# The last stage of a decoder layer cut into 670 steps, with one order over all token tiles written out for every engine, norms and quotients on ScalarE, and its loads issued behind the first gathers

## The chip, the cores and the metric

The kernel runs on one core of a Trainium2 chip. A core has a matrix engine (TensorE, in the profile PE, with its weight loads as PEld), a vector engine (VectorE, DVE), an engine for activation functions (ScalarE, ACT), a general engine (GpSimd, POOL) and one that mostly issues transfers (SyncE, SP). Each works through its own list of instructions strictly in order; they wait for one another through semaphores. Transfers are issued by SP, ACT and POOL and are carried out by 16 DMA engines that all queues share.

The metric is device time in microseconds (us) of one launch, as the median of several runs. The span is the part of one profiled launch from its first to its last instruction.

## What is computed

One decoder layer on 1024 tokens (4 sequences of 256) of width 256. After a Mamba block and a mixture of experts, three additions with a layer norm each follow:

```
x = layernorm(x + moe(x));  x = layernorm(x + cross_attention(x, ctx));  x = layernorm(x + ffn(x))
# cross attention: 16 heads of 128, 64 keys
q = rmsnorm(x @ Wq, gq);  k = rmsnorm(ctx @ Wk, gk);  v = ctx @ Wv
out = softmax(q k^T / sqrt(128)) v @ Wo
# ffn, 704 wide, with fp8 rounding of x, of the weights and of t
qx, sx = fp8(x[:, idx] / rowmax);  g, u = qx Wg^T, qx Wu^T;  t = silu(g) * u;  y = fp8(t[:, idx2]) Wd^T
```

The kernel folds Wq with the keys into one matrix M for each batch, so that scores come straight from x, and folds the values with Wo, so that the attention output is one product too. The projection x @ Wq is still done, for the norms of q alone.

## The kernel before

Tokens lie in 8 tiles of 128 rows (one row on each partition), in `x_sb`. The stages before the last one are untouched: the Mamba block with its scan (to about 430 us), the folding of keys and the routing, and the mixture of experts, which runs 23 slots of 128 rows and stores each slot's rows in the memory tensor `ys_d` (L1167). SP issues those stores, ACT the last two.

Inside the last slot the pools of the last stage are opened (L1188 to L1203). There SP is given, in this order: the context (`cT_v`), the parts of Wv and Wo for half of the heads (L641 to L647), the whole of Wq (`wq_sb`, 2 MB, L1202) and M of batch 0 (`mb`, 1 MB, L1203). Half of the folded values were computed during the scan and parked in memory (`vw_d`). The other half is computed now by `prep_v` (products `p_vT` at L657 and `p_vw` at L669, copied out by ACT).

Then POOL issues two gathers for each tile, of its two expert rows (`yg`, L1240), with the transfers of the stage between them: the parked values after tile 1 (L1246), the FFN weights after tile 3 (L1215 to L1218), M of batch 1 after tile 5 (L1253). POOL's transfers use eight semaphores in turn, so that the ninth can be issued only when the first has landed.

Each tile goes through five steps in code:

- `combine` (L1231): DVE adds the two gathered rows times their gates to x, and `layernorm` (L73 to L76) follows: statistics, `rsqrt_mean` (two small DVE instructions at L64 and L65 and a square root on ACT at L66) and the scaling on DVE (L76).
- `stage_scores`: x is transposed (L1274, copied out by ACT, L1275). Four projections with Wq (L1280) are squared by ACT (L1285) and summed by DVE (L1286) for the q norm (`rq`, L64 to L66 and L1291). Two products with M give the scores (L1295), which DVE scales (L1302). The softmax follows on whole tiles of 128x1024: maximum on DVE (L1305), subtraction on POOL (L1306), exponential on ACT (L1307), sum and reciprocal on DVE (L1308, L1309), multiplication on POOL (L1310).
- `stage_attend`: transposes (L1321), copies (L1324), eight products with the values (L1327), addition (L1330), layer norm.
- `stage_up`: POOL masks x (L1347). `quantize` takes the row maximum (L1338), scales (L1340), and `round_fp8` rounds to fp8 steps (two DVE instructions, L81 and L84, two POOL instructions, L85 and L86). Transposes (L1351, L1353) and the products `p_gu` with gate and up weights in two halves (L1361) follow; DVE scales both (L1366), ACT does the silu (L1368), DVE multiplies (L1369).
- `stage_down`: quantize again on 704 columns, transposes (L1378), copies (L1381, L1382), the products `p_fo` (L1386), DVE adds (L1391, L1392), layer norm, store (L1394).

The loop runs the tiles in a pipeline: step i does the scores of tile i, the attention of tile i-1, the up part of i-2 and the down part of i-3. Inside this loop a scheduler of the framework decides the order in which each engine gets the instructions; in the parts before it, and in the head of this stage, the order is that of the code (`manual_schedule`). Working tiles are double buffered; PSUM has four small buffers (`ps`) and two large ones (`pw`, shared by scores and `p_gu`).

Of the kernel before, what the change touches and what calls it, by code (L numbers as in the profile page):

```python
# [11 lines left out]
I32 = mybir.dt.int32  # L12
# [34 lines left out]


@with_exitstack
def decoder_kernel(  # L50
# [16 lines left out]

    def layernorm(buf, t, pool):

        st = pool.tile([P, 6], F32, tag="ln_st", name="ln_st", bufs=2)  # L70
        mv = pool.tile([P, 2], F32, tag="ln_mv", name="ln_mv", bufs=2)
        rs = pool.tile([P, 1], F32, tag="ln_rs", name="ln_rs", bufs=2)
        nc.vector.bn_stats(st, buf[:, t, :])  # L73
        nc.vector.bn_aggr(mv, st)
        rsqrt_mean(rs, mv[:, 1:2], 1, EPS_LN)
        nc.vector.tensor_scalar(buf[:, t, :], buf[:, t, :], mv[:, 0:1], rs, sub, mult)  # L76
# [52 lines left out]
    )  # L129
    a_neg = const.tile([P, NC * N], F32, name="a_neg")  # L130
# [506 lines left out]
    def prep_v(vp, groups, put):  # L637


        cT = vp.tile([P, B * S], F32, name="cT_v")  # L640
        nc.sync.dma_start(cT, ctxT)  # L641
        ws = {}
        for q in groups:
            wt = vp.tile([P, HALF], F32, tag="wv_t", name="wv_t", bufs=len(groups))
            nc.sync.dma_start(wt, wv[:, q * HALF : (q + 1) * HALF])
            w2 = vp.tile([P, GQ, D], F32, tag="wo_t", name="wo_t", bufs=len(groups))
            nc.sync.dma_start(w2, wo[q * HALF : (q + 1) * HALF, :].rearrange("(h p) d -> p h d", p=P))  # L647
            ws[q] = wt, w2
        ps = yield
        yield  # L650
        for q in groups:
            wt, w2 = ws.pop(q)
            vT = vp.tile([P, GQ, B * S], F32, tag="vT", name="vT")
            for j in range(0, GQ, 2):
                pt = ps.tile([P, HALF], F32, tag="ps", name="p_vT")
                for o in range(2):
                    nc.tensor.matmul(  # L657
                        pt[:, o * B * S : (o + 1) * B * S], wt[:, (j + o) * HD : (j + o + 1) * HD], cT,
                        start=True, stop=True,
                    )  # L660
                yield
                nc.scalar.copy(vT[:, j : j + 2, :].rearrange("p h s -> p (h s)"), pt)
            for j in range(GQ // 2):
                for b2 in range(B // 2):
                    pt = ps.tile([P, HALF], F32, tag="ps", name="p_vw")
                    for b in range(2):
                        for o in range(2):
                            bb = 2 * b2 + b
                            nc.tensor.matmul(  # L669
                                pt[o * S : (o + 1) * S, b * D : (b + 1) * D],  # L670
                                vT[:, 2 * j + o, bb * S : (bb + 1) * S], w2[:, 2 * j + o, :],
                                start=True, stop=True,
                            )
                    yield
                    put(2 * b2, q * (GQ // 2) + j, pt.rearrange("p (b d) -> p b d", d=D))
# [18 lines left out]
    with tc.manual_schedule(engines={ET.PE, ET.DVE, ET.Activation, ET.Pool}):  # L694
# [4 lines left out]
        for i, (h, c0, n) in enumerate(SL):  # L699
# [14 lines left out]
            if i == M + 2:  # L714
# [9 lines left out]
                early_values = prep_v(vp, range(2), park)  # L724
                next(early_values)
# [12 lines left out]
            if i == M + 2:  # L738
                early_values.send(ps1)
# [361 lines left out]
    with ExitStack() as sctx, tc.manual_schedule(engines={ET.PE, ET.DVE, ET.Activation, ET.Pool}):  # L1101
# [70 lines left out]
        for s in range(NSLOT + 1):  # L1172
# [13 lines left out]
            if s == NSLOT - 1:  # L1186
# [7 lines left out]
                mbs = [kvl.tile([P, KD, H * S], F32, tag="mb", name=f"mb{b}", bufs=2) for b in range(2)]  # L1194
# [3 lines left out]
                late_values = prep_v(  # L1198
                    vp, range(2, H // GQ), lambda b, pr, v: nc.scalar.copy(vw_sb[:, b : b + 2, pr, :], v)
                )  # L1200
                next(late_values)
                nc.sync.dma_start(wq_sb, wq.rearrange("(k p) c -> p k c", p=P))  # L1202
                nc.sync.dma_start(mbs[0], m_d[0].rearrange("p k h s -> p k (h s)"))  # L1203
# [9 lines left out]
    def load_ffn():  # L1213
        for j in range(2):
            nc.gpsimd.dma_start(wgu[j], wgu_d[j])  # L1215
            nc.gpsimd.dma_start(wdn[j], wdn_d[j])
        nc.gpsimd.dma_start(sgu_row, sgu_d.unsqueeze(0).to_broadcast([P, 2, I]))
        nc.gpsimd.dma_start(sdn_row, sdn_d.unsqueeze(0).to_broadcast([P, D]))  # L1218
# [3 lines left out]
    with ExitStack() as xctx:  # L1222
        wk2 = xctx.enter_context(tc.tile_pool(name="wk2", bufs=2, side="right"))
        ps = xctx.enter_context(tc.tile_pool(name="psX", bufs=4, space=PSUM))
        pw = xctx.enter_context(tc.tile_pool(name="psW", bufs=2, space=PSUM))
        ygs = {}

        def combine(t):
            if t < NT:
                for j in range(2):  # L1230
                    nc.vector.scalar_tensor_tensor(  # L1231
                        x_sb[:, t, :], ygs.pop((t, j)), g2[:, j, t : t + 1], x_sb[:, t, :], mult, add
                    )
                layernorm(x_sb, t, wk2)

        with tc.manual_schedule(engines={ET.PE, ET.DVE, ET.Activation, ET.Pool}):
            for t in range(NT):
                for j in range(2):
                    y = ygs[t, j] = wk2.tile([P, D], F32, tag="yg", name="yg", bufs=2 * NT)
                    nc.gpsimd.indirect_dma_start(  # L1240
                        out=y, out_offset=None, in_=ys_d,
                        in_offset=bass.IndirectOffsetOnAxis(ap=yrow_i[:, j, t : t + 1], axis=0),
                    )

                if t == 1:
                    nc.gpsimd.dma_start(  # L1246
                        vw_sb[:, :, 0 : H // 4, :].rearrange("p b h d -> p b (h d)"),
                        vw_d.rearrange("b p h d -> p b (h d)"),
                    )
                if t == 3:  # L1250
                    load_ffn()
                if t == 5:
                    nc.gpsimd.dma_start(mbs[1], m_d[1].rearrange("p k h s -> p k (h s)"))  # L1253
            late_values.send(ps)
            for _ in range(8):
                next(late_values)
            combine(0)
            for _ in range(3):
                next(late_values)
            combine(1)  # L1260
            run(late_values)
        mb_of = dict(enumerate(mbs))

        def load_batch(b):
            mb_of[b] = kvl.tile([P, KD, H * S], F32, tag="mb", name="mb", bufs=2)
            nc.sync.dma_start(mb_of[b], m_d[b].rearrange("p k h s -> p k (h s)"))

        def stage_scores(t):

            mb = mb_of[t * P // L]  # L1270
            x1T = wk2.tile([P, KD, P], F32, tag="x1T", name="x1T")
            pt = ps.tile([P, HALF], F32, tag="ps", name="p_x1T")
            for k in range(KD):
                nc.tensor.transpose(pt[:, k * P : (k + 1) * P], x_sb[:, t, k * P : (k + 1) * P], ident)  # L1274
            nc.scalar.copy(x1T.rearrange("p k t -> p (k t)"), pt[:, 0 : KD * P])  # L1275
            ssq = wk2.tile([P, H], F32, tag="ssq", name="ssq")
            for q in range(H // GQ):
                pq = ps.tile([P, HALF], F32, tag="ps", name="p_q")
                for k in range(KD):
                    nc.tensor.matmul(  # L1280
                        pq, x1T[:, k, :], wq_sb[:, k, q * HALF : (q + 1) * HALF],
                        start=(k == 0), stop=(k == KD - 1),
                    )
                q2 = wk2.tile([P, HALF], F32, tag="q2", name="q2")
                nc.scalar.activation(q2, pq, AF.Square)  # L1285
                nc.vector.tensor_reduce(  # L1286
                    ssq[:, q * GQ : (q + 1) * GQ], q2.rearrange("p (h d) -> p h d", d=HD), AX.X, add
                )
            rq = wk2.tile([P, H], F32, tag="rq", name="rq")
            rsqrt_mean(rq, ssq, HD, EPS_A)  # L1290
            nc.vector.tensor_scalar_mul(rq, rq, 1.0 / math.sqrt(HD))  # L1291
            psc = pw.tile([P, 2, HALF], F32, tag="pw", name="p_sc")
            for c in range(2):
                for k in range(KD):
                    nc.tensor.matmul(  # L1295
                        psc[:, c, :], x1T[:, k, :], mb[:, k, c * HALF : (c + 1) * HALF],
                        start=(k == 0), stop=(k == KD - 1),
                    )
            v = wk2.tile([P, H, S], F32, tag="v", name="v")
            full = [P, H, S]  # L1300
            st = wk2.tile([P, 2, H], F32, tag="st", name="st")
            nc.vector.tensor_tensor(  # L1302
# [94 lines left out]
        for i in range(NT + 3):  # L1397
            if i < NT:
                if i % 2 == 0 and 2 <= i // 2 + 1 < B:
                    load_batch(i // 2 + 1)  # L1400
# [78 lines left out]
```

## Time and profile before

| | |
|---|---|
| median of 3 runs | 846.73 us (846.08 to 849.98) |
| the profiled execution | 845.77 us, of which its span 843.6 us |
| PE, DVE, ACT, POOL busy over the span | 81%, 67%, 40%, 46% |
| last `ys_d` store issued | 610.4 us |
| first gather issued | 619.2 us |
| first projection of tile 0 | 631.7 us |
| last attention product of tile 7 ends | 805.8 us |
| span ends | 843.6 us |

A line of a timeline holds the start and the length in us, the engine, the source line, the instruction, its output and inputs, how many, and in brackets the idle time before it with what ended it. A line of windows holds a stretch, its length and the busy time of each engine in it, with the granted TensorE clock behind it (1.00 is full speed) and the share of the DMA engines.

### The profile page before, as it was taken

What the parts mean: (1) busy time and instruction counts of PE and PEld (TensorE: products, weight loads), DVE (VectorE), ACT (ScalarE), POOL (GpSimd) and SP (SyncE); (2) the same over time, 40 slices, a digit from 0 to 9 for tenths busy, and PEclk for the clock granted to TensorE, in tenths of its full rate; (3) what the DMA queues carried; (4) which work ended last, traced back from release to release, by engine and by line L of the source; (5) the groups of instructions that cost most, each with busy time, mean ns of one, the idle gap of its engine ahead of it and who ended that gap; (6) DMA issues with size and microseconds to landing.
All of it is one profiled execution on the core that took longest, in us unless ns stands there. A gap on an engine that the chain in (4) does not pass through costs nothing.

```text
span 843.6 us, 8099 instructions
## 1 busy us (share of the span) xinstructions
PE 683.3 (81%) x2449; PEld 379.0 (45%) x2449; DVE 563.2 (67%) x959; ACT 341.2 (40%) x564; POOL 391.2 (46%) x286
## 2 busy tenths in 40 slices
PE   3968877777666985846999999999959898889963
PEld 1533343334333443534555655655624454555531
DVE  4468799998889894564335454456227678788885
ACT  3386654755633533322212211211233455555533
POOL 7039977899766970022012332222045334344451
PEclk9999998999897998878999999999979999999985
DMA  4023222343941526963022554331566101000000
GB/s 155 1 72 84 99 73 65 88 131 118 307 123 50 162 87 219 399 225 110 26 67 23 66 54 50 60 50 45 167 248 248 50 1 50 7 6 7 8 6 19
DMA packets 57579, 80.75 MB, mean 96 GB/s; under 512 B 16033, under 2 KB 37281, under 8 KB 56769
## 3 DMA queue, kind: packets, MB, share of 16 engines
q1 hardware_dynamic: 49360, 62.21, 23.7%
q0 software_dynamic: 3632, 12.78, 7.6%
q10 hardware_dynamic: 4544, 5.24, 1.8%
q8 instruction: 21, 0.34, 0.2%
q14 instruction: 22, 0.17, 0.1%
HBM read 66.45 MB, written 13.77 MB: 95 GB/s over the span
## 4 chain that ended last, share of the span: by engine, by line
PE 46%; DVE 25%; POOL 11%; ACT 6%; issue 5%; DMA 5%; SPq 0%; POOLq 0%; ACTq 0%; DVEq 0%
PE p_gu L1128 12%; PE p_hTb L1158 7%; PE py L692 5%; DVE hs L702 5%; POOL dbx L597 4%; PE p_q L1280 3%; DVE hc L710 2%; PE p_gu L1361 2%; PE p_m L831 2%; DMA mb<-m_d 2%; PE p_cv L269 2%; POOL v L1306 1%; DVE ssq L1286 1%; DMA wk_t<-in_wk_dram 1%; PE p_hTa L1146 1%
## 5 line engine op out<-in xcount | busy, mean ns | idle before, releaser
L702 DVE TENSOR_TENSOR_SCAN hs<-da,dbx 128x1024 f32<-128x1024 f32 x64 | 145.6, 2281 | 20.3 <-POOL dbx L597 10.3
L597 POOL TENSOR_TENSOR dbx<-dtx,bB 128x1024 f32<-128x1024 f32 x64 | 149.5, 2358 | 20.2 <-DVE dtx L385 11.0
L692 PE MATMUL py<-hc,ident 128*128 128x512 f32 x256 | 132.5, 646 | 3.8 <-POOL hc L733 3.8
L1128 PE MATMUL p_gu<-w,xT 128*128 x276 | 119.3, 570 | 2.0 <-ACT xT L1118 2.0
L589 ACT ACTIVATE da<-dt,a_neg 128x510 f32<-128x510 f32 x128 | 87.7, 689 | 42.9 <-DVE hs L702 40.7
L692 PEld LDWEIGHTS py<-hc,ident 128*128 128x128 f32 x256 | 52.0, 205 | 99.8 <-issue 88.4
L1128 PEld LDWEIGHTS p_gu<-w,xT 128*128 128x128 f32 x276 | 50.0, 194 | 44.2 <-issue 34.9
L1158 PE MATMUL p_hTb<-w2r,hT 128*128 (+1 forms) x276 | 67.8, 387 | 0.0
L608 PE MATMUL pC<-bc,sel 96*128 96x512 bf16 x50 | 20.1, 401 | 56.3 <-DVE hc L710 55.5
L710 DVE TENSOR_TENSOR hc<-hs,pC 128x1024 f32<-128x1024 f32 x50 | 61.1, 1221 | 4.7
L1280 PE MATMUL p_q<-wq_sb,x1T 128*128 128x512 f32 x128 | 59.0, 615 | 4.0 <-ACT x1T L1275 3.5
L1158 PEld LDWEIGHTS p_hTb<-w2r,hT 128*128 128x128 f32 (+1 forms) x276 | 50.4, 189 | 18.4 <-issue 7.8
L1139 DVE TENSOR_TENSOR h<-sg,p_gu 128x704 f32<-128x704 f32 x23 | 20.4, 887 | 42.5 <-ACT sg L1137 42.5
L1147 ACT COPY hT<-p_hTa 128x512 f32<-128x512 f32 x23 | 13.5, 585 | 83.1 <-PE p_hTa L1146 76.0
L924 POOL DMA_INDIRECT xs<-flat_d,tok_i x23 | 22.6, 983 | 43.4 <-PE p_xT L1116 29.0
L85 POOL TENSOR_TENSOR wgu<-wgu,w_m 128x512 f32<-128x512 f32 (+1 forms) x6 | 7.6, 1267 | 71.3 <-DVE w_m L84 71.3
L1280 PEld LDWEIGHTS p_q<-wq_sb,x1T 128*128 128x128 f32 x128 | 24.5, 196 | 33.9 <-issue 27.7
L1154 DVE COPY hT<-p_hTb 128x128 f32<-128x128 f32 (+1 forms) x46 | 11.1, 282 | 42.3 <-PE p_hTb L1151 42.3
L733 POOL TENSOR_TENSOR hc<-hs,cB 128x1024 f32<-128x1024 f32 x14 | 32.9, 2351 | 11.9 <-issue 8.0
L1361 PE MATMUL p_gu<-wgu,xqT 128*128 128x352 bf16 x128 | 25.8, 367 | 10.5 <-ACT xqT L1353 10.5
L1285 ACT ACTIVATE q<-p_q 128x512 f32<-128x512 f32 x32 | 18.9, 593 | 35.9 <-PE p_q L1280 28.4
L1240 POOL DMA_INDIRECT yg<-ys_d,yrow_i x16 | 15.5, 969 | 38.3 <-DMA mb<-m_d 32.6
(332 smaller groups left out, 1265.7 us busy)
## 6 DMA issues: line engine op xcount, KB each, us to landing
bB<-b_d SPq DMA_DIRECT2D x64, 256.0 KB, 3.2
w<-in_w1T_dram SPq DMA_DIRECT2D x2, 2816.0 KB, 23.3
w<-in_w3T_dram SPq DMA_DIRECT2D x2, 2816.0 KB, 30.2
w2r<-in_w2T_dram SPq DMA_DIRECT2D x8, 640.0 KB, 7.8
m_d<-mst SPq DMA_DIRECT2D x8, 512.0 KB, 4.0
cB<-b_d SPq DMA_DIRECT2D x14, 256.0 KB, 3.5
mb<-m_d SPq DMA_DIRECT2D x3, 1024.0 KB, 4.8
ys_d<-y SPq DMA_DIRECT2D x21, 128.0 KB, 1.7
```

Source lines behind the costliest of these rows:

```text
L589: nc.scalar.activation(das[i % 2][:, j, :, 1:], dt[h][:, c, :].rearrange("p (b l) -> p b l", l=L)[:, :, 1:], AF.Exp, scale=a_neg[:, c * N ...
L597: nc.gpsimd.tensor_tensor(dbxs[i], dtx[h][:, c0 : c0 + 2, :], bBs.pop(i).unsqueeze(1).to_broadcast(two), mult)
L692: nc.tensor.matmul(ys[i][j], ident, hc[:, j, :], start=(n == 0), stop=(n == N - 1))
L702: nc.vector.tensor_tensor_scan(hs, das[i % 2].rearrange("p c b l -> p (c b l)"), dbxs.pop(i).rearrange("p c t -> p (c t)"), 0.0, mult, add,)
L710: nc.vector.tensor_tensor(hcs[i], hv, pcs.pop(i).unsqueeze(1).to_broadcast(two), mult)
L733: nc.gpsimd.tensor_tensor(hcs[i], hv, cBs.pop(i).unsqueeze(1).to_broadcast(two), mult)
L924: nc.gpsimd.indirect_dma_start(out=xs[s], out_offset=None, in_=flat_d, in_offset=bass.IndirectOffsetOnAxis(ap=tok_i[:, s : s + 1], axis=0),)
L1128: nc.tensor.matmul(pt[:, c, 0:w], x[:, k, :], w13[k][:, bass.DynSlice(ex[s], 1), o : o + w].rearrange("p e i -> p (e i)"), start=(k == 0), ...
L1139: nc.vector.tensor_tensor(hs[s], g, v[:, I : 2 * I], mult)
L1158: nc.tensor.matmul(po, hT[:w, i, :], w2r[:w, i, bass.DynSlice(ex[s], 1), :].rearrange("p e d -> p (e d)"), start=(i == 0), stop=(i == NI - 1),
L1280: nc.tensor.matmul(pq, x1T[:, k, :], wq_sb[:, k, q * HALF : (q + 1) * HALF], start=(k == 0), stop=(k == KD - 1),)
L1361: nc.tensor.matmul(pg[:, g, 0:HI], xqT[:, k, :], wgu[j][:, k, g, hs], start=(k == 0 and j == 0), stop=(k == KD - 1 and j == 1),)
```

## The change

Only the last stage changes, and what it needs set up. The loop over tiles is replaced by 670 steps. A step has an engine, an assumed length, the steps it follows and the buffers it uses. `Weave.order` plays the engines through once on the host: again and again it takes the step that can start first (within 0.037 us, the one with the lowest due time in `PLAN` plus the tile's `STARTS`), books its engine for its length and its buffers. An ACT step that needs another function table is charged 0.327 us. The resulting order is emitted under `manual_schedule`, so it is the order in which each engine gets its instructions. The steps of one tile:

- `both`: for tiles 0 and 1 two DVE instructions as before; from tile 2 on ACT multiplies the gathered rows by their gates (`gates`) and POOL adds them in two instructions.
- Norms (`ln0`, `ln1`, `ln2`): DVE statistics; the square root on ACT with eps as its bias; reciprocal and one small instruction on DVE; the scaling of x on ACT, no longer on DVE.
- `rq`: square root straight on the sums on ACT, then one DVE reciprocal.
- The softmax is done in halves of 8 heads, each with its own steps `v`, `max`, `sub`, `exp`, `sum`, `div`, `aT`, `av`.
- `x_f`, `t_f` (the quotients of the quantization) move from DVE to ACT. The scaling of the up half (`s_up`) moves from DVE to POOL, and so does the output's (`y_add`), after ACT has scaled it (`y`). Tile 7 keeps the POOL part of all this on DVE.
- The loads of Wq (in two halves) and of M of batch 0 go from SP to POOL, behind the two gathers of tile 0; the FFN weights and M of batch 1 move forward, behind the gathers of tiles 2 and 3.

```
+    "ps": 4, "pw": 2, "yg": 6, "ln": 4, "x1T": 2, "q2": 2, "nq": 3, "v": 4, "st": 4, "aT": 3, "x_f": 2, "xq": 2,
+    "sx": 4, "xqT": 2, "gu": 4, "tb": 3, "t_m": 2, "tq": 2, "s2": 4, "tT": 2, "y": 2      # buffers of each kind
-                nc.sync.dma_start(wq_sb, wq.rearrange("(k p) c -> p k c", p=P))
-                nc.sync.dma_start(mbs[0], m_d[0].rearrange("p k h s -> p k (h s)"))
...
+        for t in range(NT):
+            for j in range(2):
+                yg[t, j] = Buf("yg")
+                ld["yg", t, j] = w(f"yg.{t}", POOL, 1.25, gather(t, j, yg[t, j]), (), (yg[t, j],), lands=3.5, plan=next(turn))
+            if t == 0:
+                for k in range(KD):
+                    ld["wq", k] = load("wq", wq_sb[:, k, :], wq[k * P : (k + 1) * P, :], ())
+                ld["mb", 0] = load("mb", load_of(0), m_d[0]..., (), (mb_of[0],))
+            if t == 1:
+                ld["vw"] = load("vw", ...)
+            if t == 2:      # wgu 0, wgu 1, sgu
+            if t == 3:      # wdn 0, wdn 1, sdn, mb 1
...
+            if t < 2:
+                s = w(f"both.{t}", DVE, 1.0, both, got, ys, plan=at("both"))
+            else:
+                s = w(f"gates.{t}", ACT, 0.84, gates, got, ys, plan=at("both"))
+                s = w(f"both.{t}", POOL, 1.5, both_added, (s,), ys, plan=at("both"))
+            s = norm(t, 0, s, at("both"))
...
+    # in norm: the last of its four steps
-        nc.vector.tensor_scalar(buf[:, t, :], buf[:, t, :], mv[:, 0:1], rs, sub, mult)
+            return w(f"ln{stage}_out.{t}", ACT, 0.42,
+                lambda: nc.scalar.activation(x, x, AF.Identity, scale=b.tile[:, 7:8], bias=b.tile[:, 8:9]), (s,), (b,), plan=at)
...
-                nc.vector.tensor_tensor(gu, pg[:, :, 0:HI], sgu_row[:, :, hs], mult)
-                nc.scalar.activation(s, gu[:, 0, :], AF.Silu, scale=sx[:, 0:1])
-                nc.vector.scalar_tensor_tensor(tb[:, hs], gu[:, 1, :], sx[:, 0:1], s, mult, mult)
+                s = w(f"g_out.{t}", DVE, 0.46, ... pg.tile[:, 0, 0:HI], sgu_row[:, 0, hi], mult
+                s = w(f"silu.{t}", ACT, 0.59, ... AF.Silu, scale=sx.tile[:, 0:1]), (s,), (gu, sx), "silu", ...
+                s = w(f"s_up.{t}", eng, 0.5 if late else 0.9, ... pv.tensor_tensor(gu.tile, gu.tile, sgu_row[:, 1, hi], mult)
+                halves.append(w(f"tb.{t}", DVE, 0.58, ... pg.tile[:, 1, 0:HI], sx.tile[:, 0:1], gu.tile, mult, mult
...
-            nc.vector.tensor_scalar_mul(f, src, sc[:, 1:2])
+            s = w(f"t_f.{t}", ACT, 0.75, lambda: nc.scalar.activation(tb.tile, tb.tile, AF.Copy, scale=s2.tile[:, 1:2]), ...
...
-            nc.vector.tensor_tensor(y, po[:, 0:D], sdn_row, mult)
-            nc.vector.scalar_tensor_tensor(x_sb[:, t, :], y, sx[:, 0:1], x_sb[:, t, :], mult, add)
+                s = w(f"y.{t}", ACT, 0.42, ... nc.scalar.activation(y.tile, bo.tile[:, 0:D], AF.Copy, scale=s2.tile[:, 0:1] ...
+                s = w(f"y_add.{t}", POOL, 1.5, add_on_pool, (s, ld["sdn"]), (y,), plan=at("fo"))
```

The order that comes out, first as each engine gets it at the beginning of the stage (the number is the tile; `wgu`, `sgu`, `wdn`, `sdn` are FFN weights and scales, `val` a piece of the folded values; `[T]` marks a table load on ACT):

```
POOL yg.0 yg.0 wq wq mb yg.1 yg.1 vw yg.2 yg.2 wgu wgu sgu yg.3 yg.3 wdn wdn sdn mb yg.4 yg.4 both.2 both.3
     yg.5 yg.5 yg.6 yg.6 both.4 sub.0 yg.7 yg.7 both.5 both.6 sub.0 div.0
ACT  val x8 [T] ln0_sqrt.0 val ln0_out.0 val val x1T_out.0 ln0_sqrt.1 val ln0_out.1 gates.2 q_sq.0 x1T_out.1 q_sq.0
     gates.3 q_sq.1 q_sq.0 ln0_sqrt.2 ln0_out.2 gates.4 ln0_sqrt.3 ln0_out.3 q_sq.0 rq_sqrt.0 q_sq.1 x1T_out.2 gates.5
PE   val x11 x1T.0 val q.0 x1T.1 q.0 q.1 q.0 sc.0 sc.0 q.0 q.1 x1T.2 q.1 sc.2 q.2 sc.2 q.2 q.2 q.2 q.1 sc.1 aT.0 aT.0
```

and at its end, from the first `gu.4`:

```
PE   gu.4 gu.4 xqT.5 av.7 fo.3 gu.5 xqT.6 gu.5 fo.2 xqT.7 gu.6 gu.6 tT.4 fo.4 gu.7 gu.7 tT.5 fo.5 tT.6 fo.6 tT.7 fo.7
ACT  [T] silu.4 xqT_out.5 silu.4 x_f.6 y.3 [T] ln1_sqrt.7 xqT_out.6 t_f.4 ln1_out.7 ln2_sqrt.3 [T] silu.5 silu.5 x_f.7
     ln2_out.3 y.2 xqT_out.7 t_f.5 silu.6 silu.6 tT_out.4 [T] ln2_sqrt.2 y.4 t_f.6 ln2_out.2 [T] silu.7 tT_out.5 silu.7
     [T] ln2_sqrt.4 y.5 tT_out.6 t_f.7 ln2_sqrt.5 ln2_out.4 y.6 ln2_out.5 tT_out.7 ln2_sqrt.6 ln2_out.6 ln2_sqrt.7 ln2_out.7
DVE  tb.4 x_ex.6 res.7 ln1_stat.7 tb.4 t_sc.4 g_out.5 ln1_sc.7 ln2_stat.3 g_out.5 xm.7 x_sc.7 ln2_sc.3 t_ex.4 x_ex.7
     x_rd.7 tb.5 tb.5 t_sc.5 g_out.6 g_out.6 t_ex.5 tb.6 ln2_stat.2 tb.6 t_sc.6 ln2_sc.2 g_out.7 t_ex.6 g_out.7 s_up.7 tb.7
     ln2_stat.4 s_up.7 tb.7 t_sc.7 ln2_sc.4 ln2_stat.5 t_ex.7 ln2_sc.5 t_rd.7 ln2_stat.6 ln2_sc.6 y.7 ln2_stat.7 ln2_sc.7
POOL s_up.4 s_up.4 x_rd.6 y_add.3 s_up.5 s_up.5 t_rd.4 y_add.2 s_up.6 s_up.6 t_rd.5 y_add.4 t_rd.6 y_add.5 y_add.6
```

ACT gets 29 table loads from the first square root of the stage on; before it got 33.

## The prediction

> **What bounds the kernel now.** I read the page first, then the windows of the last stage, its PE timeline, the waits, and POOL's and ACT's timelines around its head.
>
> ```profile
> span 843.6 us, 8099 instructions
> PE   3968877777666985846999999999959898889963
> PEclk9999998999897998878999999999979999999985
> ...
> 631.70:805.80 174.10, 155.77 (x596) 88.95 (x596) 138.74 (x307) 90.60 (x145) 73.13 (x57) 0.96 0.13 48
> 805.80:843.60 37.80, 17.40 (x90) 9.46 (x90) 23.54 (x56) 11.24 (x20) 14.24 (x11) 0.69 0.04 14
> ```
>
> From 631.7 to 805.8 PE is the bound: 155.8 of 174.1 us busy (first pair of numbers), DVE 138.7, ACT 90.6, POOL 73.1. The last 37.8 us are a drain: PE is busy 17.4 us, at a clock of 0.69.
>
> ```profile
> 631.72 9.16 PE L1280 MATMUL p_q<-wq_sb,x1T 128*128 128x512 f32 x16 [0.51 <-issue]
> 645.00 7.13 PE L1280 MATMUL p_q<-wq_sb,x1T 128*128 128x512 f32 x16 [0.46 <-ACT x1T L1275]
> 802.03 3.72 PE L1327 MATMUL p_av<-vw_sb,aT 128*128 128x256 f32 x16 [0.37 <-ACT aT L1324]
> 818.26 4.88 PE L1361 MATMUL p_gu<-wgu,xqT 128*128 128x352 bf16 x16 [0.46 <-ACT xqT L1353]
> PE p_gu L1361 <- ACT xqT L1353: 10.5, 8, 2.3
> PE p_fo L1386 <- ACT tT L1381: 5.7, 3, 2.8
> ```
>
> The same 16 projections take 7.13 us warm and 9.16 after an idle stretch; `p_gu` takes 2.56 warm (at 808.6) and 4.88 in the drain. So idle PE is paid for twice. The two waits are the largest of PE within the tile loop.
>
> ```profile
> 610.43 0.33 ACTq L1167 DMA_DIRECT2D ys_d<-y  x1
> 619.17 0.95 POOL L1240 DMA_INDIRECT yg<-ys_d,yrow_i  x1 [32.56 <-DMA mb<-m_d]
> 632.51 0.54 POOL L1216 DMA_DIRECT2D wdn<-wdn_d  x1 [1.00 <-DMA vw_sb<-vw_d]
> 652.17 0.60 ACT L1285 ACTIVATE q<-p_q 128x512 f32<-128x512 f32 x1 [1.12 <-PE p_q L1280]
> 652.78 1.28 ACT L1307 ACT_TABLE_LOAD   x1
> 654.08 1.06 ACT L1307 ACTIVATE v<-v 128x1024 f32<-128x1024 f32 x1
> ```
>
> The first gather starts 8.7 us after the last store, while Wq and M (3 MB on SP) occupy the DMA engines. A POOL transfer waits for the one eight places ahead. A table load costs 1.28 us, with no gap around it.
>
> **PE's work is unchanged.** One tile, by warm rows of the PE timeline: projections 7.13, scores 3.43, attention products 3.72, their transposes 1.05, x transposed 0.30, `xqT` 0.28, `gu` 2.56, `tT` 0.62, `fo` 1.58: 20.67, eight tiles 165.4 us. Before, 12.2 of these lie behind the last attention product, so 153.2 fill 174.1 us: 20.9 lost to waits and cold clock. I call end = S + work up to the last attention product + loss + drain, where S is the time at which an unbroken PE stream would have begun. Before: 631.7 + 153.2 + 20.9 + 37.8 = 843.6.
>
> **The head, S.** With Wq and M off SP, the last store can land about 2 us after 610.4 (other `ys_d` stores on SP: median 1.7); the two gathers of tile 0 issue from 612.5 to 615. From the first gather to the end of the first norm it is 7.7 us now (626.8), so x of tile 0 is ready by about 621. Wq issues at 615, moves from 617.7 (the 2 MB of `vw` also started 2.7 us after issue) at the 400 GB/s that the DMA row shows from 627 to 643, and is there at 623: q.0 could begin 8.7 us earlier than now. But the order ties it to later gathers on the same POOL queue. After 3 MB of Wq and M, yg.1 lands at 626; after 2 MB of parked values, yg.2 at 632; after 2.1 MB of FFN weights yg.3 at 638; yg.4 at 643.5. ACT has `gates.2` ahead of the first `q_sq.0`, so nothing of q.0 is squared until 632.9; PE has x1T.1 behind one q.0 and q.1 behind x1T_out.1 (634). `gates.3` holds ACT to 638.9 and `gates.4` to 644.4. Also wdn waits for `vw` eight places ahead, and `both.2` stands behind yg.4, which holds POOL to about 639. Walking on, PE has done 6 projections and 2 scores (14.1 us) at 644.5 and loses 1.3 after it: S = 644.5 - 14.4 + 1.3 = 631.4; I take 632 for `gates.7`. Ends: 626 if the landings come six us earlier, 635 if each gate adds a stall of one us.
>
> **The middle.** PE work up to the last attention product is 165.4 less what now follows it: fo.3, gu.5, xqT.6, fo.2, xqT.7, gu.6, tT.4, fo.4, gu.7, three more tT and three more fo: 20.2. So 145.2. The other engines, whole stage, by rows:
> - ACT: per tile 7.8 us of steps as before (four squares at 0.59, eight heads' exponentials twice at 0.59, copies, silu) plus 2.1 for three norms (0.2 + 0.50, the row of ACT's scaled copy 128x256), x_f 0.45, t_f 0.76 (the 128x704 silu row), y 0.45, gates 0.9: about 104 with the values; 29 table loads at 1.28 are 37. Sum 141 (106 before).
> - DVE: 16.2 per tile, 7.5 more for tile 7, 2 for `both`: 139 (167 before).
> - POOL: 13.5 for seven tiles (halves of the softmax 1.04 each, the row of 128x512; t_rd 3.36), `both` 9, gathers 20, loads 6: 130 (98 before).
>
> All stay below PE's 165, at 70 to 75% between the head and the drain. Covered steps therefore cost nothing; the cover is PE's next work, which the order supplies (av.3, sc.4 and q.5 stand between one gu and its fo), and gu now comes at least one product behind its xqT, which takes most of the 10.5 us wait away. What is late next: `silu` then `s_up` on POOL then `tb` hold a `pw` buffer some 5 us where one DVE instruction held it; POOL's t_rd in front of s_up adds up to 3.4. And two-port waits stay: the q norm's L64 took 0.16 to 1.49 us (median 0.68) against 0.17 in idle times of POOL, and POOL is now busier. The 32 exponent instructions of the quantizations pay it still (t_m: mean 0.72 against 0.51), the norms no longer. Loss: at least 3 (cold starts alone), at most the 20.9 of now unless a rival below holds; I take 8, nearer the low end since the two largest waits go.
>
> **The drain.** With av.7 ending at 0, walked by the order and the rows: res, statistics, a table load and the square root of tile 7 end at 3.6; xqT.6 and t_f.4 keep ACT until ln1_out.7 at 5.2; xm, x_sc, x_f (behind both silu.5 at 8.0), x_ex, x_rd end at 9.8. PE has run dry at 6.1 and gets xqT.7 at 9.9. tb.5 frees `pw` at 10.4 and 11.0 for gu.6; t_rd.4 and y_add.2 hold POOL to 14.1, s_up.6 to 16.2, so tb.6 and gu.7 come at 17 to 22, on a cold clock. tb.7 at 25, t_sc.7, t_f.7, t_ex.7, t_rd.7 at 31.5; tT.7, tT_out.7 and a cold fo.7 to 36; then y, norm and store as at present (5.6 from the end of `p_fo` to the end of the span) to 41. One table load runs ahead of what it waits for (in the present drain, one at 802.48 does): 40. Bounds: 34 (DVE's 29 us behind av.7 plus 5) and 44. It is no shorter than now because four tiles' FFN remain where two did.
>
> **Sum.** 632 + 145.2 + 8 + 40 = 825.2. The profiled execution took 2.2 more than its span, so 827.4 against its 845.77; the median of the runs is 1.0 above that execution, so **828**.
>
> **A rule against a row.** "ScalarE: Activation LUTs" of the Trainium skill, section What ACT_TABLE_LOAD costs, puts a switch at about 1.28 us for the load and 1.38 for a drain, 2.66 in all. The load agrees with the trace; the drain does not show: the load at 652.78 begins as the square ends and the exponential starts 1.30 later. By the page ACT's 29 switches would be 77 us and its sum some 181, above PE's 165, and ACT the bound; by the row 141.
>
> **Rivals.**
> - *Better cover*: landings early (S 626), loss 4, drain 36: 811.2, so 814. For it: every engine has room. Against: the gates on ACT.
> - *Table loads through PE (slower)*: the order charges 0.33 for a switch that takes 1.28. If each of the 24 loads ahead of the drain arrives 0.96 late on a path for which PE waits, loss grows by 23: 848.2, so 851. It decides once 19 of the 24 pass through (18.4 / 0.96). For it: ACT is at 75% and in order. Against: four `ps` and four `v`, `st`, `gu` buffers let PE run ahead, and a load may run early.
> - *Little gained*: the gates stall the head (S 638) and half of the loads pass through: 842.7, so 845.
>
> **How the numbers follow.** Chances: forecast 0.66, better cover 0.18, table loads 0.10, little gained 0.06. The likeliest gives 828. Its own bounds, not all at one end, make 816 to 841; 811 to 843 takes in most of the better case and leaves out about 0.18. A change within 0.5% (842.5 to 851, about what a measurement of this kernel can tell from none) holds 0.05 of the last case and 0.03 of the slow one: 0.08. The rest of the slow case is slower by more: 0.07. Faster: 0.85.
>
> **What would show it.** First gather near 612.5; q.0 near 623 but its second projection after 629, with ACT's `gates.2` waiting for a DMA until about 632; PE idle below 10 us up to av.7; av.7's end near 785; PE waiting for xqT.7 and tT in the drain of about 40 us; 29 table loads of 1.28. It is wrong if ACT's squares trail PE's projections through the middle (table loads), or if gathers land long before 632 and PE streams from 624.

## The result, and the profile after

The changed kernel takes 843.9 us (median of 20 runs, 840.65 to 850.77) against 846.56 for the kernel before beside it: a ratio of 0.9976, interval 0.9954 to 0.9999. The gain of 0.24% is at the edge of the noise, and by the bound of 0.5% it is no change; 828 was forecast, and 811 to 843 as the range. The profiled execution took 842.04 us with a span of 840.3.

The page of the changed kernel (span, PE's busy tenths and granted clock), and its windows from the first projection to the end of the last attention product (792.4) and from there to the end of the span:

```profile
span 840.3 us, 8206 instructions
PE   3977877867676986745999999999978996998944
...
622.10:792.40 170.30, 148.76 (x542) 83.68 (x541) 108.98 (x252) 105.11 (x184) 90.09 (x98) 0.94 0.18 65
792.40:840.30 47.90, 25.32 (x148) 14.39 (x146) 35.47 (x79) 25.08 (x46) 24.78 (x23) 0.70 0.05 17
```

PE starts 9.6 us earlier than before (622.1 against 631.7) and ends its last attention product 13.4 us earlier (792.4 against 805.8); 1.3 us of both are the stages ahead, whose last product of the experts ended at 608.4 instead of 609.7. Then the drain takes 47.9 us, where it took 37.8. In the terms of the forecast, the span after is S 630.4 + work 145.2 + loss 16.8 + drain 47.9 = 840.3. S comes from the head's last stall: it ends at 647.25, with 16.8 us of work done. The forecast was 632 + 145.2 + 8 + 40 = 825.2. So the head came out as walked (1.6 us less), and the loss (8.8 more) and the drain (7.9 more) took the gain.

These terms add up lengths of rows, and a row runs on for some 0.16 us beside the next one (in the second order's rows further down, eight projections last 3.70 us and the next product starts 3.54 after them). So 165.4 us is too much for eight tiles: by the usual distance from start to start in unbroken stretches (0.429 us for a projection, 0.149 for a `gu` product) they come to 151.9. Counted from start to start, PE lost 34.4 us (time beyond those distances) between its first projection and the end of its last attention product before, and 35.0 in the changed kernel, 25.8 of them behind 647.25. The forecast's term of loss shows 20.9 and 16.8 of that. Forecast and result are counted alike, so the 8.8 between them stand.

PE's waits in the stage:

```profile
PE ps L1600 <- DVE xq L1584: 7.8, 1, 7.8
PE ps L1672 <- ACT tT L1662: 5.6, 4, 2.6
PE ps L1454 <- ACT x_sb L1416: 5.2, 2, 2.7
PE pw L1617 <- DVE tb L1641: 5.1, 1, 5.1
PE pw L1503 <- ACT x1T L1459: 2.8, 1, 2.8
```

The waits of `p_gu` for `xqT` (10.5 us before) are gone, as forecast. In their place stand one wait for tile 7's quantized x (7.8), waits for `tT` (5.6, as before), and one for a `pw` buffer that `tb` holds (5.1).

The head, on ACT and PE:

```profile
622.13 2.59 PE L1469 MATMUL ps<-wq_sb,x1T 128*128 128x512 f32 x4
630.24 0.91 ACT L1437 ACTIVATE yg<-yg,g 128x256 f32<-128x256 f32 x2 [2.83 <-DMA yg<-ys_d,yrow_i]
631.05 0.57 ACT L1476 ACTIVATE q<-ps 128x512 f32<-128x512 f32 x1
636.16 0.51 ACT L1437 ACTIVATE yg<-yg,g 128x256 f32<-128x256 f32 x1 [3.78 <-DMA yg<-ys_d,yrow_i]
647.25 3.68 PE L1503 MATMUL pw<-mb,x1T 128*128 128x512 f32 x4 [2.81 <-ACT x1T L1459]
```

The first projection runs at 622, but its square (`q`, L1476) stands on ACT behind `gates.2` (L1437), which waits until 630.24 for the gathered rows of tile 2; `gates.3` waits again until 636.16. That is the tie to later gathers of the forecast.

### The profile page after: what moved, and what is told of

Same layout as the page of the kernel before. It is cut to its first block, busy times and chain, and to the rows that moved or that the text cites. A ratio compares the mean times of both kernels' runs of the same rounds, so it can differ in the third digit from the quotient of the medians.

```text
span 840.3 us, 8206 instructions
## 1 busy us (share of the span) xinstructions
PE 679.4 (81%) x2449; PEld 376.3 (45%) x2449; DVE 542.8 (65%) x922; ACT 369.4 (44%) x627; POOL 417.2 (50%) x336
## 4 chain that ended last, share of the span: by engine, by line
PE 45%; DVE 24%; POOL 10%; ACT 10%; DMA 6%; issue 4%; DVEq 0%; ACTq 0%; POOLq 0%; SPq 0%
PE p_gu L1234 12%; PE p_hTb L1264 7%; PE py L800 5%; DVE hs L810 5%; POOL dbx L694 4%; PE ps L1469 3%; DVE hc L818 2%; PE p_m L937 2%; PE p_cv L366 2%; PE pw L1503 1%; DMA wgu<-wgu_d 1%; DMA wk_t<-in_wk_dram 1%; PE pw L1617 1%; DVE v L1512 1%; PE p_hTa L1252 1%
## 5 line engine op out<-in xcount | busy, mean ns | idle before, releaser
L1469 PE MATMUL ps<-wq_sb,x1T 128*128 128x512 f32 x128 | 60.3, 611 | 2.1 <-ACT x1T L1459 2.1
L1481 DVE TENSOR_REDUCE nq<-q 128x4 f32<-128x512 f32 x32 | 21.5, 678 | 27.0 <-ACT q L1476 26.7
L1469 PEld LDWEIGHTS ps<-wq_sb,x1T 128*128 128x128 f32 x128 | 24.6, 199 | 29.6 <-issue 25.5
L1503 PE MATMUL pw<-mb,x1T 128*128 128x512 f32 x64 | 33.3, 654 | 5.1 <-ACT x1T L1459 2.8
L919 POOL TENSOR_TENSOR ks<-ks,k_ss 128x512 f32<-128x512 f32 x8 | 8.1, 1037 | 49.4 <-ACT k_ss L169 49.4
```

Of the source, the lines that this page charges most:

```text
L1469: nc.tensor.matmul(bq.tile, x1T.tile[:, k, :], wq_sb[:, k, q * HALF : (q + 1) * HALF], start=(k == 0), stop=(k == KD - 1),)
L1481: lambda q=q, q2=q2: nc.vector.tensor_reduce(nq.tile[:, 0, q * GQ : (q + 1) * GQ], q2.tile.rearrange("p (h d) -> p h d", d=HD), AX.X, add) ...
L1503: nc.tensor.matmul(sc.tile[:, c, :], x1T.tile[:, k, :], mb.tile[:, k, c * HALF : (c + 1) * HALF], start=(k == 0), stop=(k == KD - 1),)
```

## Experiments

Lengths of the stage below run from the end of PE's last product of the experts to the end of the span (231.9 us in the changed kernel, 233.9 before): the stages ahead of it end anywhere from 606.7 to 613.1 in these profiled executions, and this takes their spread out.

**Twenty-nine table loads as one.** The slower rival put the loss down to them. Square root and SiLU become tanh, which shares the exponential's table; nothing else moves, and the values are no longer the layer's.

```
-    nc.scalar.activation(b.tile[:, 7:8], b.tile[:, 7:8], AF.Sqrt, bias=eps_ln)
+    nc.scalar.activation(b.tile[:, 7:8], b.tile[:, 7:8], AF.Tanh, bias=eps_ln)
     # likewise rq_sqrt and silu
```

> The changed kernel with the square roots and silus of the last stage replaced by tanh, which shares the table of the exponential: the same instructions, sizes and order, but one table load in the stage instead of 29 (the values are then not the layer's). Theory A (the gain went to PSUM buffers held through long chains and to DVE instructions that stand still while GpSimd works; table loads lie on PE's path in a few places only: the two within the 5.1 us stall at 709.7 and about three in the drain): 5 to 10 us less than the changed kernel's 843.9, so 834 to 839. Theory B (each load comes about one us later than the order assumed, and PE waits for most of them): at least 20 us less, so 824 or below.

Measured: 838.82 us, ratio to before 0.9915 (0.9876 to 0.9954); stage 225.3. So in this order 28 loads, 36 us of ACT, cost about 5 us of time (6.6 by the stages). They are not the bound, and the drain hardly moves (46.8).

**The up half on DVE.** The forecast named one thing to be late next: `silu`, `s_up` on POOL and `tb` hold a `pw` buffer. One DVE instruction scales both halves, as before the change, and `s_up` goes.

```
-    gu.tile, pg.tile[:, 0, 0:HI], sgu_row[:, 0, hi], mult
+    gu.tile, pg.tile[:, :, 0:HI], sgu_row[:, :, hi], mult      # gu is [P, 2, HI]
-    lambda hi=hi, gu=gu: pv.tensor_tensor(gu.tile, gu.tile, sgu_row[:, 1, hi], mult), (s,), (gu,),
+    lambda: None, (s,), (gu,),
```

> The changed kernel, in the same order, but DVE scales the gate and the up half in one instruction out of PSUM as in the kernel before, and GpSimd's scaling of the up half (s_up) is gone, so that a pw buffer is free after that instruction and not after silu, GpSimd and a further DVE instruction. Theory A: the 5.1 us stall of gu.1 on tb and the cold products behind it (about 2.3) go, and t_rd.4 starts some 1.5 us earlier in the drain: 7 to 10 us less than 843.9, so 834 to 837; DVE gets 6 us more work, which is hidden up to the drain. Theory B (the table loads set the pace): at most 2 us, 842 to 844, since the loads stay where they are.

Measured: 842.24 us, 0.9986 (0.9961 to 1.0012), stage 232.3: a miss for theory A. The time is the one that theory B named, but by the first experiment the loads cost too little for its reason. PE's timeline of this kernel at the place of the 5.1 us wait:

```profile
713.42 1.53 PE L1617 MATMUL pw<-wgu,xqT 128*128 128x352 bf16 x8 [1.96 <-DVE gu L1625]
717.36 0.40 PE L1600 MATMUL ps<-identb,xq 128*128 128x128 bf16 x2 [2.41 <-POOL xq L1584]
719.63 1.97 PE L1547 MATMUL ps<-ident,v 128*128 128x128 f32 x8 [1.87 <-POOL v L1538]
```

The wait falls to 1.96, and two others of 2.41 and 1.87 follow within 6 us. PE has only short products here, each at the end of a chain through other engines; with this chain shortened, the next two are late.

**Tile 7's rounding on GpSimd.** `x_rd.7` on DVE took 3.57 us (0.6 in the forecast). Here it runs on POOL, ahead of `t_rd.4`.

```
+        late = next(s for s in steps if s.name == "t_rd.4")
+        steps.remove(late)
+        steps.insert(1 + next(i for i, s in enumerate(steps) if s.name == "x_rd.7"), late)
...
-    lambda: rounded(xq.tile, xf.tile[:, 0], xf.tile[:, 1]), (s,), (xf, xq)
+    lambda: rounded(xq.tile, xf.tile[:, 0], xf.tile[:, 1], nc.gpsimd), (s,), (xf, xq)
```

> The changed kernel with one step moved: the rounding of tile 7's x (two additions of 128x256) runs on GpSimd ahead of the rounding of tile 4's t, where it ran on DVE beside it and took 1.77 us for each instruction against 0.42 for such an instruction with an input in PSUM. If DVE stood still for GpSimd's instruction (theory A), the two take 1.5 us on GpSimd in place of 3.5, tb.5 comes 3 us earlier, PE's wait for xqT.7 falls from 7.8 to about 5.5 and the end comes 1.5 to 3 us earlier: 841 to 842.5. If the 1.77 us are DVE's own length for two inputs in SBUF, GpSimd is still faster but its t_rd.4 is delayed by 1.5 us and the end moves by less than 1 us either way.

Measured: 841.77 us, 0.9982 (0.9948 to 1.0015). PE's wait for `xq` of tile 7 falls from 7.77 to 5.84 us and the drain from 47.9 to 45.9. So the rounding's length is worth 2 us of the drain. In the time it does not show: the stage is 231.6 against 231.9, since the last attention product ends 1.7 us later, counted from the experts' last product.

**Wq and M back on SP**, ahead of the last stores, as before the change.

```
+                nc.sync.dma_start(wq_sb, wq.rearrange("(k p) c -> p k c", p=P))
+                nc.sync.dma_start(mb_first, m_d[0].rearrange("p k h s -> p k (h s)"))
```

> The changed kernel with the loads of Wq and of M of batch 0 back on SP and ahead of the last stores, in the same order otherwise. If the head is set by the chain of landings on GpSimd's queue (theory A), the first gather moves from 611.7 to about 618, but yg.2 and later land at about the same time, since 3 MB fewer lie ahead of them: PE's unbroken stream would begin 0 to 3 us later and the time is 844 to 847. If moving the loads brought the first products forward by what the first gather gained (rival), 6 to 9 us are lost: 850 to 853.

Measured: 845.36 us, 1.0003 (0.9974 to 1.0032). The first gather falls back to 619.3 and the first projection to 629.9, yet the score product that starts the unbroken stretch comes at 650.05 instead of 647.25, with the stages ahead 1.8 us later. The loads' new place, by itself, is worth 1 to 2 us in this order (1.3 by the stages, 0.3% by the ratios, whose intervals overlap): the first projection comes 8 us earlier (6 without the stages ahead), and its square then waits for `gates.2`.

These four leave the order of the work itself. The kernel's own ordering (`Weave.order`) keeps an account of the stage: it ends at 202.5 us, where the chip took 231.9. I therefore replayed the stage with durations from the trace: each engine in its order, table loads at 1.283, DVE's two-input steps behind POOL's running one, PE at half clock behind an idle stretch, loads landing as in the trace. This is an estimate worked out of the changed kernel's rows. A first form of it ended the last norm 3 to 4 us ahead of the trace, and from single steps moved about in it came the orders below.

**The same steps in another order**; two more orders found with one price left out.

```
-        for s in self.order():
+        for s in (self.steps[n] for n in ORDER):    # ORDER: the numbers of the 670 steps
```

> The changed kernel's 670 steps, each as it is, with the same tiles and numbers of buffers, in another order. The order was found by moving single steps about and replaying the stage each time: every engine in its own order, each step with the duration that its rows in the trace of the changed kernel show, a table load at 1.28 us, a wait of VectorE's two-input steps for the instruction that GpSimd is running, TensorE at half clock behind a stretch in which it was busy for less than 0.4 of 3.4 us, the loads landing when they landed in that trace. The replay of the changed kernel's own order ends its last norm 3 to 4 us before the trace does. Theory A (what was lost, 16.8 us ahead of the last attention product and 47.9 behind it, is a matter of the order: PE's work of other tiles stands in the wrong place): the replay ends 45 us earlier, so some 797 us, 793 to 808 with the landings; the last attention product ends near 765, the drain is 28 to 36 us, PE idle there below 10. Theory B (the steps themselves cost it: the waits between four engines come back elsewhere in any order, as with the scaling of both halves on VectorE): 830 or more, drain over 42. Theory C (PE's bound is the head: landings keep PE from running ahead): between, 812 to 825, with the gain only behind the last attention product.

> As the reordered kernel, but its order was found with a table load priced at 0.33 us, as the changed kernel's own order prices it. Everything else of the replay is the same. Theory A (the price of a table load is what the changed kernel's order lacked most): replayed with 1.28 it ends 18 to 20 us after the reordered kernel, so 812 to 822 us, with more table loads than the reordered kernel's. Theory B (the loads mostly run ahead of what they wait for, whatever the order): within 4 us of the reordered kernel.

> As the reordered kernel, but its order was found without the wait of VectorE's two-input steps for GpSimd's running instruction (each takes what it takes alone). Theory A (the wait is real and costs in the order): replayed with it, it ends 9 us after the reordered kernel, so 803 to 813 us. Theory B (the wait is only a way in which the profile shows it, or is hidden): within 3 us of the reordered kernel.

| kernel | us | ratio to before | stage | av.7 ends | drain | table loads |
|---|---|---|---|---|---|---|
| changed kernel | 843.9 | 0.9976 (0.9954 to 0.9999) | 231.9 | 792.4 | 47.9 | 29 |
| reordered | 808.71 | 0.9615 (0.9558 to 0.9672) | 197.9 | 769.0 | 36.9 | 28 |
| blind to loads | 828.37 | 0.9809 (0.9775 to 0.9843) | 217.4 | 782.1 | 43.9 | 38 |
| blind to sharing | 812.70 | 0.9613 (0.9582 to 0.9644) | 198.8 | 764.8 | 45.8 | 23 |

The same instructions end 35 us earlier. That is theory A, although the time is 12 us above the replay and 0.7 above the range given. With a table load priced at 0.33, the order found is 20 us slower, as theory A said (18 to 20), though 828.37 itself is above its 812 to 822. Leaving out the wait for POOL costs 4 us in the medians and next to nothing in the ratio or the stage, where theory A had 9: 812.70 lies in its range only because both kernels ran above the replay. That is nearer to theory B, and no difference that can be measured, although the wait itself is plain in the rows (last section). The replay's first form had this wait badly placed; a second form plays both engines in the order of time. Each of these kernels is one order, so what another order found alike would take is not known.

**A second order, the tail alone, ScalarE's queue alone.** All three use the second form of the replay.

> The changed kernel's 670 steps once more, in an order found with a better replay: engines are played through in the order of time, and a two-input step of VectorE and a step of GpSimd exclude each other both ways (whichever comes second ends its own length less 0.15 us behind the other's end), as the rows of the reordered kernel's trace show it. By this replay the changed kernel's last norm ends at 838.2, the reordered kernel's at 800.5 and this one's at 793.1. Theory A (the order is the whole loss): the reordered kernel ran 8.2 us above its replay, so 801 us, 797 to 806. Theory B (what is left is landings and chains that no order takes away): no faster than the reordered kernel, 808 or more.

> The changed kernel with its first 500 steps in their old order, up to the second fo of tile 1 (776 us), and only the 170 behind it put in another order. Theory A (the drain is long because of the order in it, whatever precedes): the last attention product ends as before, near 792, the drain falls from 47.9 to 34 us, so 830 us, 826 to 834. Theory B (the drain is set by tile 7's chain through four engines, which the steps behind the last attention product cannot shorten): drain over 43, 839 or more.

> The changed kernel with ScalarE's queue alone in another order (134 of its 201 places hold another step, 28 table loads where there were 29); every other engine gets its steps exactly as in the changed kernel. Theory A (ScalarE's queue, ordered with a table load at 0.33 us, sets much of the loss): the replay ends 10.9 us earlier, so 833 us, 829 to 838, with the last attention product near 786 and a drain of 43. Theory B (only all queues together can be better, or TensorE's own order is what is wrong): within 3 us of the changed kernel, 841 to 847.

The second order takes 801.15 us, 0.9495 (0.9459 to 0.9532), 801 being expected. It beats both kernels, by 5% the one before. Its windows, and ACT and PE in its head:

```profile
622.10:756.80 134.70, 134.68 (x518) 78.78 (x517) 103.86 (x249) 100.91 (x175) 85.04 (x93) 1.00 0.21 76
...
756.80:798.10 41.30, 25.84 (x172) 15.08 (x170) 33.61 (x84) 25.18 (x54) 29.26 (x26) 0.82 0.08 26
```

```profile
622.05 3.70 PE L1500 MATMUL ps<-wq_sb,x1T 128*128 128x512 f32 x8
624.07 0.60 ACT L1507 ACTIVATE q<-ps 128x512 f32<-128x512 f32 x1 [1.32 <-PE ps L1500]
625.59 1.88 PE L1534 MATMUL pw<-mb,x1T 128*128 128x512 f32 x4
626.70 0.57 ACT L1507 ACTIVATE q<-ps 128x512 f32<-128x512 f32 x1
629.47 0.91 ACT L1468 ACTIVATE yg<-yg,g 128x256 f32<-128x256 f32 x2 [2.19 <-DMA yg<-ys_d,yrow_i]
```

From 622.1 to the end of the last attention product PE is busy for 134.68 of 134.70 us at full clock: S is 622, and 1.4 us are lost from start to start, where the changed kernel lost 35.0. The rows of tile 2 land no earlier than in the changed kernel (629.47 against 630.24); the two squares simply stand ahead of `gates.2`. The products left behind the last attention product come to 22.7 us by the forecast's rows (18.2 from start to start), and they drain in 41.4 us. By the same rows 142.7 us of work would stand in those 134.7, which is how much the rows count twice.

The tail alone: 833.81 us, 0.9867 (0.9826 to 0.9908), with the last attention product at 797.8 (its stages ahead ended 3.7 us later) and a drain of 36.0 instead of 47.9. PE's work in it is almost the same (18.9 us for 19.9, by rows); the last attention product comes 1.7 us later, counted from the experts, so the stage gains 10.2 (221.7). Theory A. ScalarE's queue alone: 839.57 us, 0.9937 (0.9913 to 0.9962), stage 227.1, drain 47.3. That lies between the theories: some 4 us come from ScalarE's queue, where the replay gave 10.9; the shorter drain that was expected (43) did not come.

**Norms and quotients back on VectorE, and the price of a load mended alone.**

```
-    lambda: nc.scalar.activation(x, x, AF.Identity, scale=b.tile[:, 7:8], bias=b.tile[:, 8:9]), (s,), (b,),
+    lambda: nc.vector.tensor_scalar(x, x, b.tile[:, 7:8], b.tile[:, 8:9], mult, add), (s,), (b,),    # step on DVE
     # likewise x_f and t_f; ORDER found anew
...
-SLACK, SWITCH = 0.037, 0.327      # the other kernel: this line alone
+SLACK, SWITCH = 0.037, 1.283
```

> The last step of the 24 norms and the quotients x_f and t_f go back from ScalarE to VectorE (40 steps; 0.32 us each, t_f 0.56, by the rows of the kernel before), and the 670 steps get an order found in the same way as the second order's, with these steps on VectorE. Theory A (where these steps run is worth little once the order suits it): the replay ends at 796.9 against 793.1, so 805 us, 801 to 811. Theory B (moving them to ScalarE is what makes a good order possible, since VectorE is the busiest engine behind TensorE): 815 or more.

> The changed kernel with one number of its own ordering changed: a table load is priced at 1.283 us instead of 0.327; the starts and ranks that the ordering uses stay. 22 table loads come out where there were 29. The ordering's own account of the stage ends at 214.6 us where it ended at 202.5 (the chip took 231.9). Theory A (the starts and ranks were fitted to the wrong price, so the price alone mends nothing): the replay ends at 842.7 against 838.2 now, so 842 to 852. Theory B (seven table loads less and a truer price are a gain by themselves): 828 to 839.

With these 40 steps on DVE: 813.57 us, 0.9644 (0.9606 to 0.9682), between the theories again. So with these steps on ScalarE the order found is 12 us better in the medians (10 in the stage); with them on DVE, a suitable order with the rest of the change still gives 30 us against the kernel before. The replay (4 us) had too low prices for them; DVE's groups in this kernel:

```profile
L1447 DVE TENSOR_SCALAR x_sb<-x_sb,ln 128x256 f32<-128x256 f32 x23 | 9.6, 425 | 0.3
...
L1679 DVE TENSOR_SCALAR tb<-tb,s 128x704 f32<-128x704 f32 x8 | 5.8, 729 | 0.0
L1622 DVE TENSOR_SCALAR x_f<-x_f,sx 128x256 f32<-128x256 f32 x8 | 4.4, 556 | 0.1
```

They were priced at 0.32, 0.56 and 0.32, some 6 us too little in all. The order was found with these prices, so how much of the 12 us is the steps' place and how much a wrong price is not shown.

The price mended alone: 852.42 us, 1.0100 (1.0074 to 1.0126), slower, with 22 loads. That is theory A (0.4 us above its range), with a cause that I had not named. ACT and PE's largest wait in it:

```profile
634.00 0.91 ACT L1437 ACTIVATE yg<-yg,g 128x256 f32<-128x256 f32 x2 [12.62 <-DMA yg<-ys_d,yrow_i]
634.92 1.28 ACT L1411 ACT_TABLE_LOAD   x1
...
PE ps L1454 <- ACT x_sb L1416: 16.8, 1, 16.8
```

The dearer load made the ordering put `gates.2` ahead of the first square root. The ordering takes a gather to land 3.5 us after its issue (`lands=3.5`); the second of tile 2, issued at 620.86 in the changed kernel, let `gates.2` start 9.4 us later. So a second wrong price decided here, and tile 0 waited for tile 2's rows.

## Why the prediction was wrong

**The head: right.** S was 630.4 for a forecast of 632 (the stages ahead ended 1.3 us earlier than before), with the first gather at 611.7 (612.5), the first projection at 622.1 (623) and ACT held by `gates.2` until 630.2 (632). What was missed is that this cost 8 us which nothing but the order asked for: the second order has S at 622, with its loads issued in the same order and tile 2's rows there at 629.5.

**The waits that were to go: right.** The 10.5 us of `p_gu` behind `xqT` went; the waits for `tT` stayed.

**Table loads: the forecast's price was right, the rival wrong as a bound.** 29 loads of 1.28 us with no drain behind them cost 5 us in place. They matter more as a wrong price in the ordering than as time on ACT (20 us between two orders found alike).

**The failing step is "Covered steps therefore cost nothing; the cover is PE's next work, which the order supplies".** The engines' sums did stay below PE's (from 622.1 on DVE was busy 144 us, ACT 130, POOL 115, PE 174), and the second order shows that a PE almost without loss was possible. But sums do not say that the work is ready in the order written. I read one place of PE's order that looked covered (av.3, sc.4 and q.5) and sized the loss at 8 instead of walking the middle as I had walked the head. It was 16.8 in the same terms, 25.8 from start to start; two holes hold 12.6 of it, and the rest is many smaller ones. The first, and the line of the second, in the changed kernel on PE, ACT and DVE:

```profile
703.20 1.35 PE L1617 MATMUL pw<-wgu,xqT 128*128 128x352 bf16 x8 [1.38 <-DVE ln L1405]
709.67 2.50 PE L1617 MATMUL pw<-wgu,xqT 128*128 128x352 bf16 x8 [5.11 <-DVE tb L1641]
770.29 3.60 PE L1503 MATMUL pw<-mb,x1T 128*128 128x512 f32 x4 [2.31 <-DVE v L1512]
...
702.83 1.28 ACT L1528 ACT_TABLE_LOAD   x1
705.26 1.28 ACT L1631 ACT_TABLE_LOAD   x1
708.03 1.28 ACT L1528 ACT_TABLE_LOAD   x1
...
708.23 0.90 DVE L1580 TENSOR_SCALAR x_f<-x_f 128x256 f32<-128x256 f32 x1
709.04 0.57 DVE L1641 SCALAR_TENSOR_TENSOR tb<-pw,sx,gu 128x352 f32<-128x352 f32 x1
```

`gu.1` needs the `pw` buffer that `tb.0` frees; `tb.0` has two table loads, POOL's softmax steps and DVE's exponents ahead of it. PE waits 1.38 and 5.11 us and then runs cold (2.50 against 1.35, and 1.97 against 1.05 for the next transposes): 8.6 us. The other hole, at 770, is a wait of 2.31 and a score product of 3.60 instead of 1.88: 4.0 us. Half clock behind idle time is what "TensorE: Matmul & The Clock Gate" of the Trainium skill, Part 1, describes, an idle window of some 3.4 us being enough. In these two places it followed gaps of 5.11 and of 2.31 us, so here a gap shorter than that window was enough, while the products behind the gap of 1.38 ran warm (1.35).

**The drain: mechanism right, sizes wrong.** Forecast 40, range 34 to 44; it was 47.9. By the steps of the walk, from the end of av.7: `x_rd.7` ended at 13.7 instead of 9.8, since `x_ex.7` took 1.52 us (0.56) and `x_rd.7` 3.57 (0.6); gu.6 then ran cold in 4.73 us; `s_up.7` took 0.83 and 1.58 (0.5), `t_rd.7` 2.24 (1.5); and fo.7 ended at 42.0 instead of 36. Tile 7's x on DVE and PE:

```profile
801.59 0.90 DVE L1580 TENSOR_SCALAR x_f<-x_f 128x256 f32<-128x256 f32 x1
806.15 0.39 PE L1600 MATMUL ps<-identb,xq 128*128 128x128 bf16 x2 [7.77 <-DVE xq L1584]
806.65 4.73 PE L1617 MATMUL pw<-wgu,xqT 128*128 128x352 bf16 x16
```

The forecast gave the wait for POOL to DVE's one-input instructions of the q norm and the exponents alone and priced tile 7's two-input steps as if POOL stood still. Moving one of them off shortened the drain by 2 us. The larger part is order again: with the tail's 170 steps in another order it is 36.0 us, and the stage 10.2 us shorter.

**The range** left 843.9 out by 0.9 us. "Little gained" (845, chance 0.06) came closest in time, by another mechanism: not the gates at S 638, but the holes of the middle and the drain. It had no rival of its own in which the covering order fails.

What stays open: how much of the gap between the two orders belongs to the price of a table load, how much to the landing of the loads (3.5 and 6 us in the ordering, about 9 for tile 2's rows) and how much to the way of ordering. The changed kernel was not ordered anew with all prices mended and its own starts and ranks fitted again.

## What to carry to other kernels

Engines that all sum to less than the bound leave room for a good order, and no more; before a forecast counts steps as covered, walk the written order once through every queue, with measured durations, to the end. An order that a program computes is as good as its prices: here its own account (202.5 us against 231.9) would have told that they were off, and mending one price without fitting the rest made it slower. When removing a wait brings nothing, look whether the next chain was late by the same amount, and then change the order rather than the chain.

## What the runs showed of the hardware

In these traces VectorE's instructions that read two SBUF tensors stand still while GpSimd runs one, and the other way about. DVE, then POOL, in the changed kernel:

```profile
802.53 1.77 DVE L1583 TENSOR_TENSOR x_f<-x_f 128x256 f32<-128x256 f32 x1
804.33 1.77 DVE L1584 TENSOR_TENSOR xq<-x_f 128x256 bf16<-128x256 f32 x1
815.84 1.29 DVE L1406 SCALAR_TENSOR_TENSOR ln<-ln 128x1 f32<-128x1 f32 x1
...
802.30 1.71 POOL L1583 TENSOR_TENSOR tb<-tb,t_m 128x704 f32<-128x704 f32 x1
804.09 1.73 POOL L1584 TENSOR_TENSOR tq<-tb,t_m 128x704 bf16<-128x704 f32 x1
815.44 1.68 POOL L1584 TENSOR_TENSOR tq<-tb,t_m 128x704 bf16<-128x704 f32 x1
```

Each DVE instruction ends 0.29, 0.28 and 0.01 us behind POOL's; the last one has a single element per partition and takes 0.16 alone. In the reordered kernel POOL waits in turn: its second half of `t_rd.3`, begun 0.11 us behind a `sub.7` of DVE, takes 2.11 instead of 1.68. The exponents' one-input instructions are held up too (`x_ex.7`: 0.59 and 0.90 us, 0.29 each at 698.0 where POOL stood still). Steps with one input in PSUM are not (`g_out` 0.47 to 0.52, `res` 0.36 to 0.42 throughout). That agrees with "SBUF — State Buffer" of the Trainium skill, SBUF: two separate sides, which calls the pair of ports that the two share an exclusive lock for the whole instruction.

A table load does not wait for what its activation waits for: in the changed kernel at least 10 of the 29 began before that input was ready, one 3.6 us before. And ScalarE's forms with two per-partition operands were dearer than the copies from which I priced them: the norm's scaling took 0.60 us (0.50), the square root with a bias 0.29 (0.20).
